# A layer of attention, state-space mixing and 32 routed experts: experts placed by token count, weights gathered by place

## The chip, the cores and the metric

The kernel runs on one core of a Trainium2 chip. The metric is device time in microseconds (us) of one execution; the time of a version is the median of its runs. Five engines work beside each other and meet at semaphores: TensorE (PE, matmuls, with its weight loads shown as PEld), VectorE (DVE), ScalarE (ACT), GpSimd (POOL) and SyncE (SP). Transfers (DMAs) are issued from the queues of SP, ACT and POOL and run on 16 shared DMA engines. Matmul results land in PSUM[...]; other tiles lie in SBUF, 128 partitions wide.

## The reference, cut to what matters

The layer adds three blocks to `x` (256 tokens x 512): attention over 4096 context tokens and itself, a state-space mixer, and a feed-forward block with a shared expert and 32 routed ones. The change lies in the routed part:

```python
scores = jax.nn.sigmoid(x @ gate_w)                      # 256 x 32
topk_w, topk_i = jax.lax.top_k(scores, 6)
topk_w = topk_w / (jnp.sum(topk_w, axis=-1, keepdims=True) + 1e-20)
combine = jnp.sum(jax.nn.one_hot(topk_i, 32) * topk_w[..., None], axis=1)
g = jnp.einsum('td,edf->tef', x, wg)                     # wg, wu: 32 x 512 x 192
u = jnp.einsum('td,edf->tef', x, wu)
act = jax.nn.silu(g) * u
routed = jnp.einsum('tef,efd,te->td', act, wd, combine)  # wd: 32 x 192 x 512
shared = jax.nn.silu(x @ sg) * (x @ su) @ sd
return routed + shared
```

A token uses 6 of the 32 experts, so 1536 rows of work are spread unevenly over them. All values are f32.

## The kernel before

**Places.** Every expert has a place of 128 rows in a scratch tensor `xg` in device memory, expert `e` at row `128 e`. Experts are worked on in 16 pairs, `n` = 0 to 15, pair `n` holding experts `2n` and `2n + 1`. If an expert has over 128 tokens, the flag `crowded` sends the kernel through a second pass over all places (the `Else` arm at its end).

**Routing.** For each token tile `t` of 128, `route` (L988) computes gate scores, the six chosen experts and the 0/1 matrix `mask`; `rows_of` (L1017) multiplies `mask` with a triangle of ones, which gives each token its rank within its expert, and from that the row it goes to. `scatter` (L1010) then sends the tile's normalised rows to `xg` with six indirect DMAs from POOL. Tile 0 goes through this while tile 1 is still in the mixer. `picks` (L1033) builds selection matrices for the first four experts (`HEAD`), whose rows are picked on PE by `ps_pick` (L1302) instead of going through `xg`. `shares` (L1039) computes the flag and the normalised weights. The shared expert (`shared_hidden`, `shared_down`) runs on PE between these steps.

**Weights.** A pair has three pieces of 128 x 1536 f32 (768 KiB): gate and up of the first expert, of the second, and both down weights. The host lays them out as one array `pairs`. Fifteen slots (five pairs, `NHELD`) hold them; they are SBUF tiles of earlier stages, filled as these come free. `load_piece(p)` (L1079) issues piece `p` from SP's queue into slot `p % 15`, as soon as PE has finished with the piece before.

**The loop over pairs** (L1337) issues, in step `n`: `gate_up(n)`, the loads of pair `n + 5`'s two gate pieces, `fetch(n + 2)` (two 128 x 512 row blocks from `xg`, on SP's queue), `turn(n + 1)` (eight 128 x 128 transposes and a copy), `down(n - 1)` with the store of its rows to `ye` from ACT's queue, the load of pair `n + 4`'s down piece, and `turn_hidden(n)`. In `gate_up`, each expert takes four f32 matmuls of 128 rows x 384 columns, then SiLU on ACT and two products on VectorE. An expert's hidden width is 192 = 128 + 64: the two 64-wide rests of a pair share one 128-wide transpose, and in `down` (L1288) they are multiplied as two matmuls of 64 partitions each.

**The end.** The last six experts (`TAIL`, pairs 13 to 15) don't go through `ye`. `weights_back` builds matrices `spread` that carry a token's weight for each place row, `spread_hidden` multiplies the hidden rows with them, and `down_into` sums the results in two PSUM banks, `total`. The results of the other experts come back by twelve indirect DMAs from POOL (`gather`, L1192) and are added on VectorE (`add`). Two last adds (L1378) and two stores end the kernel.

**What sets the order.** The program text gives an order, and a scheduler moves instructions within it as their operands become ready; each engine then runs its own stream in order. A wait therefore holds back all that is queued behind it on that engine. Clearing `xg`, `ye` and `ye2` (L515) is done during attention, in seven portions on SP's queue, with transfers pinned in program order.

Of the kernel before, what the change touches and what calls it, by code (L numbers as in the profile page):

```python
# [11 lines left out]
FP = mybir.dt.float32  # L12
# [42 lines left out]
NHELD = 5  # L55
HEAD = 4
TAIL = 6
ROUNDS = L // P
# [9 lines left out]
def perceiver_layer(ctx: ExitStack, tc: tile.TileContext, a: dict, out: bass.AP):  # L68
# [49 lines left out]

    xg = tc.dram_tile((ROUNDS * NE * P, DM), FP, name="xg")
    ye = tc.dram_tile(((NE + 1) * P, DM), FP, name="ye")  # L120
    ye2 = tc.dram_tile(((NE + 1) * P, DM), FP, name="ye2")
# [12 lines left out]
    def layer(ctx, bounded):  # L134
# [16 lines left out]
        most = keep.tile([1, 1], FP, name="most")  # L151
# [363 lines left out]
        def clear(n):  # L515

            per = -(-ROUNDS * NE // (NC - 1))
            e0, e1 = n * per, min((n + 1) * per, ROUNDS * NE)
            zeros(xg[e0 * P:e1 * P, :].rearrange("(e p) d -> p e d", p=P),
                  xn[:, 0:1, :].to_broadcast([P, e1 - e0, DM]))  # L520
            if n == 0:
                for y in (ye, ye2):
                    zeros(y[(NE - TAIL) * P:, :].rearrange("(e p) d -> p e d", p=P),
                          xn[:, 0:1, :].to_broadcast([P, TAIL + 1, DM]))
# [452 lines left out]
        def routing_memory():  # L977
            r = carve(lacc[:, 1], (P,), (P,), (NE,), (NT, NE), (NT, NE), (NT, NE), (NT, NE), (NT, NE), (NT, 8), (NT, 8),
                      (NT, TOPK), (NT, TOPK), (NT,), (NT * TOPK, NE), (FT, L))
            names = ("iota", "before", "first", "gate", "ev", "mask", "rank", "dst", "m8", "idx", "rowf", "w8", "den", "hot", "act")  # L980
# [3 lines left out]
            V.tensor_scalar(m["first"], m["iota"][:, 0:NE], float(P), None, ALU.mult)  # L984

# [31 lines left out]
        def rows_of(t):  # L1017

            mask, rank, dst, hot = m["mask"], m["rank"][:, t, :], m["dst"][:, t, :], m["hot"][:, t]
# [4 lines left out]
            V.tensor_copy(rank, pr)  # L1024

            V.tensor_scalar(dst, rank, float(P), float((NE - 1) * P), ALU.is_ge, ALU.mult)
            V.tensor_tensor(dst, dst, rank, ALU.add)
            V.tensor_tensor(dst, dst, m["first"], ALU.add)
            V.tensor_tensor(hot, hot, dst.unsqueeze(1).to_broadcast([P, TOPK, NE]), ALU.mult)
            V.tensor_reduce(m["rowf"][:, t, :], hot, AX.X, ALU.add)  # L1030
            V.tensor_copy(row[:, t, :], m["rowf"][:, t, :])
# [7 lines left out]
        def shares():  # L1039

            pr = bank("ps_most")[:, 0:NE]
            for t in range(NT):
                TE.matmul(pr, ones, m["mask"][:, t, :], start=(t == 0), stop=(t == NT - 1))
            V.tensor_reduce(most, pr[0:1, :], AX.X, ALU.max)
            V.tensor_scalar(crowded, most, float(P), None, ALU.is_gt)
# [32 lines left out]

        def load_piece(p):  # L1079
            if p < 3 * NP:  # L1080
                slots_of[p] = slots[p % (3 * NHELD)]
                nc.sync.dma_start(slots_of[p], a["pairs"][p // 3, p % 3])
# [80 lines left out]
        rows_of(0)  # L1163
# [3 lines left out]
        scatter(0)  # L1167
        load_into(wvc, wkc, ctx0)
        load_into(*w_out)
        pick, = carve(m["kv", 1], (NT * HEAD, P))  # L1170
        pick = pick.rearrange("p (t e) r -> p t e r", t=NT)
        picked, = carve(m["kv", 0], (KD, HEAD, P))
        turn()
        shared_down(0)
        route(1)
        product, turn = shared_hidden(1)
        product()
        rows_of(1)
        scatter(1)
        for t in range(NT):  # L1180
            picks(t)
        shares()
        turn()
        shared_down(1)
        actx.close()

# [21 lines left out]
        class Rounds:  # L1208


            def __init__(self, ctx, weights):
                pool = lambda name, bufs, **kw: ctx.enter_context(tc.tile_pool(name=name, bufs=bufs, **kw))
                self.r, self.weights = 0, weights
                self.e2, self.e4 = pool("e2", 2), pool("e4", 4)
                self.ps_x, self.ps_gu = pool("ps_x", 2, space=PSUM), pool("ps_gu", 2, space=PSUM)
                self.ps_t, self.ps_ye = pool("ps_t", 1, space=PSUM), pool("ps_ye", 3, space=PSUM)
                self.rows, self.xgT, self.hid, self.hidT, self.done = {}, {}, {}, {}, {}

            def fetch(self, n):
                for i in range(2):  # L1220
                    self.rows[n, i] = self.e4.tile([P, DM], FP, tag="xg", name="xg_sb")
                    r0 = (self.r * NE + 2 * n + i) * P
                    nc.sync.dma_start(self.rows[n, i], xg[r0:r0 + P, :])
# [245 lines left out]
```

## Time and profile before

| | value | how to read it |
|---|---|---|
| median of 3 runs | 1013.92 us | 1013.66 to 1014.13 |
| the profiled execution | 1013.77 us | its own device time |
| its span | 1012.0 us | first to last instruction, 9057 of them |
| PE busy | 992.4 us, 98% | matmuls overlap and their ends are modelled: busy is not peak |
| PE weight loads busy | 477.8 us, 47% | beside the matmuls |
| DVE, ACT, POOL busy | 498.6, 391.7, 152.6 us | 49%, 39%, 15% of the span |
| mean granted PE clock | 0.999 | 1 is full speed |
| DMA | 131.94 MB, mean 130 GB/s | in the expert stage, 860 to 940 us, 352 to 365 GB/s |

A line of the timeline or of the chain of waits gives the start in us from the span's start, the length in us, the engine, the line of the kernel, the operation, what it writes and reads, and how many instructions are merged in it; in brackets stands the idle time before it and who ended it. "SPq" and "ACTq" are DMA issues. The attention part fills the first 740 us, the mixer the time to about 820, routing and the shared expert the time to about 840, and the pairs of experts the rest.

### The profile page before, as it was taken

The numbers are of one execution on the slowest core, as the hardware profiler recorded it, in microseconds if no ns is written. First come the engines' busy times: TensorE is split into PE (matmuls) and PEld (weight loads), VectorE is DVE, ScalarE is ACT, GpSimd is POOL, SyncE is SP. The second block draws the span as 40 slices with busy tenths as digits, with TensorE's granted clock in tenths as the row PEclk, the third lists the DMA queues.
The fourth block names the chain that finished last, engine by engine and source line by source line (L and its number), as shares of the span: only waits on it lengthen the run. The fifth ranks groups of instructions, "written<-read, shape, count | busy, mean of one in ns | idle before, by whom it ended". The sixth has DMA issues, their size and how long they took to land.

```text
span 1012.0 us, 9057 instructions
## 1 busy us (share of the span) xinstructions
PE 992.4 (98%) x2786; PEld 477.8 (47%) x2786; DVE 498.6 (49%) x976; ACT 391.7 (39%) x862; POOL 152.6 (15%) x155
## 2 busy tenths in 40 slices
PE   7999999999999999999999999999999999999997
PEld 3444444444444444444444444444656554555554
DVE  4455555454454454454544544575886653322124
ACT  3645444343443443443443434432444431222210
POOL 4343002001101101100201200000132322000013
PEclk9999999999999999999999999999999999999999
DMA  9635045132222313303304203500254358999823
GB/s 335 214 64 169 0 146 197 32 97 80 52 47 99 83 32 114 84 17 129 83 8 138 64 0 84 156 11 0 94 189 155 114 208 321 350 358 367 310 98 116
DMA packets 136556, 131.94 MB, mean 130 GB/s; under 512 B 80401, under 2 KB 99762, under 8 KB 135346
## 3 DMA queue, kind: packets, MB, share of 16 engines
q1 hardware_dynamic: 129392, 115.71, 36.0%
q0 software_dynamic: 2208, 8.39, 2.3%
q10 hardware_dynamic: 4898, 7.16, 1.9%
q8 instruction: 24, 0.39, 0.1%
q14 instruction: 34, 0.28, 0.1%
HBM read 90.86 MB, written 40.39 MB: 130 GB/s over the span
## 4 chain that ended last, share of the span: by engine, by line
PE 95%; DVE 1%; ACT 1%; POOL 1%; DMA 1%; issue 0%; SPq 0%; ACTq 0%
PE oT L586 23%; PE scT L561 23%; PE ps_kv L358 17%; PE ps_egu L212 8%; PE ps_self L212 3%; PE ps_ye L1285 2%; PE ps_v L212 2%; PE ps_o L782 2%; PE total L1276 2%; PE ps_xbc L212 1%; PE ps_ye L1288 1%; PE ps_k L212 1%; PE xgTp L1230 1%; PE ps_out L972 1%; PE ps_yd L912 1%; DMA wkv<-in_wk_ctx_dram 1%
## 5 line engine op out<-in xcount | busy, mean ns | idle before, releaser
L577 DVE TENSOR_TENSOR lacc<-lacc,prT 128x512 f32<-128x512 f32 x256 | 182.7, 715 | 240.5 <-ACT prT L567 239.7
L567 ACT ACTIVATE prT<-scT,bq,rk 128x512 f32<-128x512 f32 x256 | 198.8, 777 | 254.7 <-PE scT L561 242.1
L561 PE MATMUL scT<-qT,kT 128*128 128x512 f32 x536 | 270.9, 592 | 0.0
L586 PE MATMUL oT<-prT,v 128*128 128x512 f32 x528 | 268.0, 592 | 0.9 <-ACT prT L567 0.9
L586 PEld LDWEIGHTS oT<-prT,v 128*128 128x128 f32 x528 | 100.1, 190 | 127.2 <-issue 115.0
L561 PEld LDWEIGHTS scT<-qT,kT 128*128 128x128 f32 x536 | 101.2, 190 | 124.6 <-issue 122.2
L190 POOL TENSOR_TENSOR rk<-pv,mhalf 128x4 f32<-128x4 f32 x32 | 32.3, 1010 | 371.1 <-DVE pv L189 371.1
L1245 DVE TENSOR_TENSOR hid<-si,ps_egu 128x128 f32<-128x128 f32 x32 | 9.2, 288 | 95.7 <-ACT si L1243 94.2
L358 PE MATMUL ps_kv<-wkv,fast 128*128 128x512 f32 x112 | 53.4, 592 | 0.0
L248 ACT ACTIVATE sq<-kraw 128x128 f32<-128x128 f32 x128 | 35.6, 278 | 45.2 <-DVE kraw L376 43.2
L358 PE MATMUL ps_kv<-wkv,ctx 128*128 128x512 f32 x112 | 52.8, 592 | 0.0
L358 PE MATMUL ps_kv<-fast,fast 128*128 128x512 f32 x112 | 52.6, 592 | 0.0
L592 DVE TENSOR_TENSOR oacc<-oT,oacc 128x512 f32<-128x512 f32 x64 | 43.7, 683 | 0.0
L1291 ACT COPY y_sb<-ps_ye 128x512 f32<-128x512 f32 x26 | 15.2, 585 | 48.8 <-PE ps_ye L1288 43.0
L358 PEld LDWEIGHTS ps_kv<-wkv,fast 128*128 128x128 f32 x112 | 21.3, 190 | 26.8 <-issue 26.8
L358 PEld LDWEIGHTS ps_kv<-fast,fast 128*128 128x128 f32 x112 | 21.3, 190 | 26.8 <-issue 21.8
L358 PEld LDWEIGHTS ps_kv<-wkv,ctx 128*128 128x128 f32 x112 | 21.3, 190 | 26.8 <-issue 23.7
L1198 POOL DMA_INDIRECT yk<-ye,row_y x12 | 12.8, 1064 | 139.0 <-DVE hid L1246 135.7
L1243 ACT ACTIVATE si<-ps_egu 128x192 f32<-128x192 f32 x32 | 10.6, 331 | 58.5 <-PE ps_egu L212 58.5
L376 DVE TENSOR_TENSOR kraw<-ps_kv,fast 128x256 f32<-128x256 f32 x42 | 17.9, 425 | 28.2 <-PE ps_kv L358 28.2
L782 PE MATMUL ps_o<-wo,qT 128*128 128x512 f32 x64 | 28.8, 592 | 0.0
L212 PE MATMUL ps_self<-wq,xT 128*128 128x512 f32 x64 | 28.1, 592 | 0.0
(298 smaller groups left out, 1120.9 us busy)
## 6 DMA issues: line engine op xcount, KB each, us to landing
xg<-xn SPq DMA_DIRECT2D x6, 2560.0 KB, 9.9
w_in<-in_pairs_dram SPq DMA_DIRECT2D x14, 768.0 KB, 6.6
ctx<-in_ctxT_dram SPq DMA_DIRECT2D x7, 1024.0 KB, 9.2
kd<-tr SPq DMA_DIRECT2D x112, 64.0 KB, 2.1
kT<-kd SPq DMA_DIRECT2D x28, 256.0 KB, 2.7
xg_sb<-xg SPq DMA_DIRECT2D x28, 256.0 KB, 6.0
ye<-y_sb ACTq DMA_DIRECT2D x26, 256.0 KB, 7.0
wkv<-in_pairs_dram SPq DMA_DIRECT2D x6, 768.0 KB, 6.5
```

What stands on the lines that cost most here:

```text
L190: return G.tensor_tensor(dst, v[:, :n], mhalf[:, :n], ALU.pow)
L212: TE.matmul(ps, lhs(k), rhs_of(k), start=(k == 0), stop=(k == KD - 1))
L248: S.activation(sq[:, h, :], raw[:, h, :], AF.Square, accum_out=ss[:, h:h + 1])
L358: TE.matmul(ps, lhs(k), rhs(k), start=(start and k == 0), stop=(k == 1), skip_group_check=True)
L561: TE.matmul(sc, kT[:, g, i * P:(i + 1) * P], qT[:, t, heads4(g), :].rearrange("p h q -> p (h q)"), start=True, stop=True)
L567: S.activation(pr, sc, AF.Exp, bias=shift, scale=SCALE if r is None else r[:, i, g:g + 1])
L577: V.tensor_tensor(la, la, pr, ALU.add)
L586: TE.matmul(outs[g, t], v[:, i, g * HD:(g + 1) * HD], pr, start=(n == 0), stop=last)
L592: V.tensor_tensor(ov, outs.pop((g, t)), ov, ALU.add)
L782: TE.matmul(m["ps_o", t], aT[:, t, h, :], wo[j][:, h % 4, :], start=(h == 0), stop=(h == NH - 1))
L1276: TE.matmul(total[t], h[:, j, t * P:(t + 1) * P], wd[:, j, :], start=(first and j == 0), stop=(last and j == 2))
L1285: TE.matmul(ps[i], h[:, i, :], wd[:, i, :], start=True, stop=False)
```

## The change

Ten experts (0 to 9, `FIXED`) keep their places, two pairs' worth of which are picked on PE as before. The other 22 are sorted by token count on the chip. The ten with most tokens take wide places of 128 rows (pairs 5 to 9), the other twelve narrow places of 64 rows (pairs 10 to 15), two of which share one block of 128 rows. Only now is it known which expert sits where, so the weights of pairs 5 to 15 are gathered by place with indirect DMAs from POOL, five per pair, and the host lays weights out by expert. A narrow pair is computed in halves of 64 stationary columns that write the lower and the upper half of one PSUM bank. A token beyond 64 in a narrow place, or 128 in another, raises `crowded`; the second pass's memory grows accordingly.

Both tiles' rows depend on the counts of all tokens, so all twelve scatters now follow `places` and `rows`, which come after the second tile's routing; `route(1)` is put ahead of `shared_down(0)`. Pair 2's `turn` is put behind `down(0)`. The constants, the sizes of `xg`, `ye` and `ye2`, and the clears follow the new places: thirteen blocks in a portion where it was ten, and a single block each for `ye` and `ye2` where it was seven.

```diff
+FIXED = 2 * NHELD
+WIDE = FIXED + 10
+HALFP = P // 2
-ROUNDS = L // P
+ZROW = WIDE * P + (NE - WIDE - TAIL) * HALFP
+MAIN = ZROW + TAIL * HALFP
...
+        def places():
+            mask, first, pos, key, keys, at, less, over = (m[n] for n in ("mask", "first", "pos", "key", "keys", "at", "less", "over"))
+            few, n, low = slice(0, NE), NE - FIXED, slice(FIXED, NE)
+            pc = bank("ps_count")
+            for t in range(NT):
+                TE.matmul(pc[:, 0:NE], ones, mask[:, t, :], start=(t == 0), stop=(t == NT - 1))
+            pp = bank("ps_count2")
+            for t in range(NT):
+                TE.matmul(pp[few, 0:16], mask[:, t, :], ones[:, 0:16], start=(t == 0), stop=(t == NT - 1))
+            V.scalar_tensor_tensor(keys, pc[:, 0:NE], float(NE), m["iota"][:, 0:NE], ALU.mult, ALU.subtract)
+            V.tensor_scalar(keys, keys, float(2 * NE), None, ALU.add)
+            V.scalar_tensor_tensor(key[few], pp[few, 0:1], float(NE), m["p"][few], ALU.mult, ALU.subtract)
+            V.scalar_tensor_tensor(key[few], key[few], float(2 * NE), m["free"][few], ALU.add, ALU.mult)
+            V.tensor_scalar(at[few, 0:n], keys[few, low], key[few], None, ALU.is_gt)
+            V.tensor_reduce(pos[few], at[few, 0:n], AX.X, ALU.add)
+            V.tensor_scalar(at[few], ident[few, few], pos[few], None, ALU.mult)
+            V.tensor_scalar(less[few, 0:n], m["iota"][few, 0:n], pos[few], None, ALU.is_equal)
+            ps = bank("ps_place")
+            TE.matmul(ps[:, 0:NE], ones[few], at[few], start=True, stop=True)
+            TE.matmul(ps[:, NE:NE + n], number[few], less[few, 0:n], start=True, stop=True)
+            V.tensor_copy(at, ps[:, 0:NE])
+            V.tensor_copy(expert, ps[:, NE:NE + n])
...
+        def rows():
+            rank, dst = m["rank"], m["dst"]
+            by_tile = lambda ap: ap.unsqueeze(1).to_broadcast([P, NT, NE])
+            V.tensor_tensor(dst, rank, by_tile(m["less"]), ALU.add)
+            V.tensor_scalar(dst, dst, float(P), None, ALU.is_ge)
+            V.tensor_tensor(dst, dst, by_tile(m["over"]), ALU.mult)
             V.tensor_tensor(dst, dst, rank, ALU.add)
+            V.tensor_tensor(dst, dst, by_tile(m["first"]), ALU.add)
+            for t in range(NT):
+                hot = m["hot"][:, t]
+                V.tensor_tensor(hot, hot, dst[:, t].unsqueeze(1).to_broadcast([P, TOPK, NE]), ALU.mult)
+                V.tensor_reduce(m["rowf"][:, t, :], hot, AX.X, ALU.add)
+                V.tensor_copy(row[:, t, :], m["rowf"][:, t, :])
...
+        def gather_weights(slot, n, j):
+            def rows(out, src, c):
+                G.indirect_dma_start(out=out, out_offset=None, in_=src.rearrange("e p n -> (e p) n"),
+                                     in_offset=bass.IndirectOffsetOnAxis(ap=place[:, c:c + 1], axis=0))
+            s = 2 * n - FIXED
+            if j < 2:
+                rows(slot, a["gu"], s + j)
+            else:
+                for i in range(2):
+                    rows(slot[:, i * DM:(i + 1) * DM], a["down"], s + i)
+                rows(slot[:, 2 * DM:], a["down_rest"], NE - FIXED + s // 2)
...
-                nc.sync.dma_start(slots_of[p], a["pairs"][p // 3, p % 3])
+                (load_weights if p < 3 * NHELD else gather_weights)(slots_of[p], p // 3, p % 3)
...
-        rows_of(0)
+        ranks(0)
         product, turn = shared_hidden(0)
         mamba_out(1)
         product()
-        scatter(0)
...
         turn()
+        route(1)
         shared_down(0)
-        route(1)
         product, turn = shared_hidden(1)
         product()
-        rows_of(1)
-        scatter(1)
+        ranks(1)
+        places()
+        rows()
+        for t in range(NT):
+            scatter(t)
         for t in range(NT):
             picks(t)
         shares()
+        weight_rows()
         turn()
         shared_down(1)
...
+            def gate_up_halves(self, n):
+                ps = self.ps_gu.tile([P, 2 * FE], FP, tag="gu", name="ps_egu")
+                xT = self.xgT.pop((n, 0))
+                w = [self.weights[3 * n + i].rearrange("p (k n) -> p k n", k=KD) for i in range(2)]
+                for k in range(KD):
+                    for i in range(2):
+                        TE.matmul(ps[self.half(i)], xT[:, k, self.half(i)], w[i][:, k, :], start=(k == 0), stop=(k == KD - 1))
+                si = self.e2.tile([P, FE], FP, tag="si", name="si")
+                S.activation(si, ps[:, 0:FE], AF.Silu)
+                hid = self.hid[n] = self.zeroed[n % 2]
+                V.tensor_tensor(hid[:, 0:P], si[:, 0:P], ps[:, FE:FE + P], ALU.mult)
+                for i in range(2):
+                    h = self.half(i)
+                    self.done[n] = V.tensor_tensor(hid[h, P + i * REST:P + (i + 1) * REST], si[h, P:FE], ps[h, FE + P:], ALU.mult).ins
...
+            def down_halves(self, n, to):
+                wd = self.weights[3 * n + 2].rearrange("p (j n) -> p j n", j=3)
+                h = self.hidT.pop(n)
+                ps = self.ps_ye.tile([P, DM], FP, tag="ye", name="ps_ye")
+                for i in range(2):
+                    TE.matmul(ps[self.half(i)], h[:, 0, self.half(i)], wd[:, i, :], start=True, stop=False)
+                TE.matmul(ps, h[:, 1, :], wd[:, 2, :], start=False, stop=True)
...
+            def spread_halves(self, n, by):
...
+                for i in range(2):
+                    TE.matmul(whole[i][:, 0, :], h[self.half(i), 0:P], by[self.half(i)], start=True, stop=True)
+                TE.matmul(whole[1][:, 1, :], h[:, P:2 * P], by, start=True, stop=True)
...
-                main.gate_up(n)
+                wide = 2 * n < WIDE
+                (main.gate_up if wide else main.gate_up_halves)(n)
...
-                if FIRST <= n + 1 < NP:
+                if FIRST <= n + 1 < NP and n + 1 > FIRST:
                     main.turn(n + 1)
                 if 0 < n <= LAST:
-                    main.down(n - 1, ye)
+                    (main.down if 2 * (n - 1) < WIDE else main.down_halves)(n - 1, ye)
+                    if n + 1 == FIRST:
+                        main.turn(n + 1)
```

Three more functions are used above. `ranks` is the first half of the old `rows_of`. `weight_rows` turns the sorted experts into row numbers for the gathers, in five steps on VectorE. `turn_hidden_halves` transposes two 128-wide blocks instead of three; the hidden tiles of narrow pairs are two zeroed tiles whose unused corners stay zero. In `weights_back` the matrices are built for two narrow places together: six transposes where there were twelve, after a selection of ranks and weights by place on VectorE.

## The prediction

> **What bounds the kernel now.** I began with the busy table and the 40 slices: TensorE (PE) is busy 98% of the span at a granted clock of 0.999, but the DMA row also stands at 8 and 9 in slices 33 to 37, so an average can't say which of the two sets the pace of the expert stage. The windows by stage settle it. The columns of the next line are the stretch, its length, busy time of PE, weight loads, VectorE (DVE), ScalarE (ACT) and GpSimd (POOL), then clock, DMA share and GB/s.
>
> ```profile
> 880.00:900.00 20.00, 20.00 (x83) 11.43 (x83) 7.61 (x22) 4.38 (x11) 0.00 (x0) 1.00 0.97 352
> ```
>
> PE has no hole, the DMA engines hardly one, POOL does nothing. The chain that ended last, followed in order of time, gives one pair of experts:
>
> ```profile
> 861.77 5.16 PE ps_egu L212 x16
> 866.93 0.87 PE xgTp L1230 x8
> 867.81 1.72 PE ps_ye L1285 x4
> 869.53 1.06 PE ps_ye L1288 x4
> 870.59 0.48 PE hidTp L1252 x3
> ```
>
> The chain never leaves PE: 9.29 us a pair (861.77 to 871.06), and the same lines return up to pair 12. Each f32 matmul is two records, so 5.16 us is 16 of 0.322 us. In the same 9.29 us the queues move 3 weight pieces of 768 KiB, two row blocks in and two out of 256 KiB, 3.41 MB: 367 GB/s, what the DMA engines give at a share near 1. Yet PE waits for none of it, because weights come five pairs ahead: pair 15's gate pieces are issued at 940 and 943, and its gate-up starts at 989, a lead of over 40 us.
>
> The third view is the timeline around the routing, where the path leaves PE:
>
> ```profile
> 821.45 0.96 POOL L1013 DMA_INDIRECT xg<-xn,row  x1 [0.30 <-issue]
> 822.44 0.58 POOL L190 TENSOR_TENSOR rs<-pv,mhalf 128x1 f32<-128x1 f32 x1
> ...
> 843.86 0.96 POOL L1013 DMA_INDIRECT xg<-xn,row  x1 [0.30 <-issue]
> 848.96 1.75 SPq L1223 DMA_DIRECT2D xg_sb<-xg  x4
> ```
>
> The layernorm's factor stands behind a scatter of the first token tile; the last scatter ends at 844.82 and rows may be fetched 4.1 us later. PE first needs them at 857.48, so there is cover.
>
> **Does the routing fit the places?** Routing the reference's own inputs gives counts that sum to 1536. Of the 22 sorted experts the tenth largest has 63 rows, so the largest narrow one has 43; no fixed or wide one has over 103. Nothing overflows 64 or 128, and the second pass isn't taken.
>
> **The six narrow pairs (10 to 15), PE alone.** The halves of gate-up have half the stationary columns each and write different halves of one bank. No row of the trace splits the array by columns; the nearest splits it by rows, L1288: 4 records of 512 columns in 1.06 us, where L1285 takes 1.72 for four whole ones. Two perfect lanes would take 0.86, so a change of tiling costs 0.20.
> - Gate-up: 5.16 becomes 2.58 + 0.20, and some 0.07 for the lanes' offset: 2.85. Saved 2.31 x 6 = 13.9.
> - Row transposes (one block, not two): 0.87 to 0.435, x 6: 2.6.
> - Down, pairs 10 to 12: 1.72 + 1.06 = 2.78 becomes 1.06 for the halves and 0.86 for the shared rest: 1.92. x 3: 2.6.
> - Hidden transposes: two for three, 0.16 x 3: 0.5.
> - Spreading, pairs 13 to 15: 1.06 + 0.86 = 1.92 becomes 0.43 + 0.20 + 0.43 = 1.06. x 3: 2.6.
> - Spread transposes: six for twelve of 1.6 us: 0.8.
> Sum: **23.0 us**.
>
> [...] both column halves use all rows. The trace's row: whole loads of 190 ns ("PEld LDWEIGHTS" of L212) use all rows too, and their matmuls still follow each other every 0.322 us. [...] With no concurrency at all it is 5.16 + 0.20. I take the row. Below 2.58 two lanes can't go.
>
> Other engines keep up: in a narrow step of some 5.5 us ACT has 0.33 + 0.58 and under 0.48 for the hidden copy, DVE about 1.4 (0.68 + 0.29 + two of 0.21). The next pair's transposed rows have the down product and the hidden transposes, 2.2 us, to be copied in 0.68.
>
> **Routing.** `places` adds two counts and a placement on PE in place of `ps_most` (4 records, 0.45 us): 12 records for 4, +0.9. Its vector work, all after the second tile's mask, is some 18 dependent steps at 0.18 to 0.22 on 32 columns before `rows`, which has five steps on 64 columns and two times 0.85 (L1029 to L1031). I make it 6.1 us and 1.5 of PE round trip: 7.6 from mask to last row, where it was 832.36 to 837.27, 4.9. Against that, route(1) now goes ahead of shared_down(0) (2.84), and no scatter stands before the layernorm factor on POOL: VectorE hands it over at 821.07 and POOL starts at 822.44, so 1.3 us go and PE's wait at L1064 (0.9) with it, -1. So rows are ready at 837 to 840, I say 838.5.
>
> Then **all twelve scatters** stand in one run: 12 x 1.26 = 15.2 us, ending 853.7 instead of 844.8. Plus 4.1 the fetch is at 857.8, plus 2.6 to 3.5 landing (2.6 is the fastest fetch of the trace) the rows are there at about 861. Besides, VectorE between 828 and 838 must do some 11 us in 10, with the picks that `ps_pick` waits for: +1 (0 to 3). The change moves pair 2's transposes behind down(0). Gate-up(0), at 846.62 before, comes at 846.62 + 0.9 - 1 + 1 = 847.5, and 5.16 + 5.64 + 2.78 later, at 861.1, the transposes are due: level with the rows. Where two chains meet, either can be late: **stall 1 us**, between 0 and 5 (rows ready at 842.5, nothing gained by the reordering).
>
> **Weights move from SP's to POOL's queue.** Per pair five gathers, each blocking on its slot; behind a blocked one stand only further weight gathers, since the y gathers come after the last of them. SP keeps the row fetches, no longer behind 768 KiB loads (median landing 6.0). The first gathers wait for the scatters, 853.7 instead of 850.8: inside the lead. The near row is the y gather:
>
> ```profile
> 980.48 0.99 POOL L1198 DMA_INDIRECT yk<-ye,row_y  x1 [135.66 <-DVE hid L1246]
> 981.78 0.96 POOL L1198 DMA_INDIRECT yk<-ye,row_y  x1 [0.30 <-ACT si L1243]
> 983.05 0.95 POOL L1198 DMA_INDIRECT yk<-ye,row_y  x1 [0.31 <-issue]
> ```
>
> They start every 1.3 us without waiting for each other's landing: 5 x 1.27 = 6.3 us a pair, under 9.29. Were POOL's time to grow with the bytes (6 KB rows against 2 KB), it is 2 x 3.2 + 3 x 1.27 = 10.2 a pair, 112 us for eleven, done at 967. Pair 10 starts at 937.57 + 0.9 - 1 + 1 + 1 = 939.5, and the steps after it take 6.4, 5.5, 5.5, 6.3 and 9.5 by the numbers above: pair 15 needs its weights at 973. [...] The row shows the starts overlapping, so I count nothing.
>
> The clears grow from ten blocks to thirteen (3.4 MB), the first shrinks from 6.2 to 3.9; attention, which shows no wait for 6.2, hides them. POOL's two memsets of hidden tiles (nearest row: its 128x512 add, 1.27 us), `weight_rows` and the four extra steps of `shares` come after the scatters' rows and ahead of the first gather only, in its lead.
>
> **The end.** After down(12) at 974.26, PE has 32.06 us left. Of these go 2 x 2.31 (pairs 14, 15), 0.43 and three spreads of 0.86: 24.4 left. The y gathers hang on the same point: copy and store 5.3 (one block's copy fewer than 6.2), 16.1 of issue, 2 to land, 0.9 to add: 24.3. They were 6.5 us early; now they are level with PE, +0.7 (0 to 2).
>
> **Sum.** -23.0 + 0.9 - 1 + 1 + 1 + 0.7 = -20.4: span 991.6. Around the profiled span lie 1.77 us (1013.77 against 1012.0), and that execution stands 0.15 below the median of 1013.92. Forecast **993.5 us**.
>
> **Rivals.**
> - *The halves overlap, but badly, or the stall is long* ([...] rows at 842.5 or later, +4 and more: 998 to 1004). For: no row with column halves; DVE is full around 830. Against: the row-split row. 20%.
> - *No concurrency by columns*: gate-up 5.36, down 2.78, a spread 1.49. Left are 2.6 + 0.5 + 1.3 + 0.8 - 1.2 = 4.0 against 2.6 of the other terms: 1012.5, about nothing. Against it is again L1288, which does run two at once. 4%.
> - *Gathered weights bind: slower.* Place: POOL's queue from 853.7 on. Eleven pairs, 25.95 MB, must be in by pair 15's gate-up; before, that stood at 989. It gets slower than before when the gathers bring under 192 GB/s (25.95 MB in 135 us), 12.3 us a pair. [...] For it: these gathers are not in the trace, 55 of them are new. Against: the overlapping starts; q0 moved 8.39 MB in 2.3% of the span, at full rate. 8%.
> - *It doesn't do what it says*, the overflow pass running after all: the counts exclude it. 1%.
> The forecast itself, 987.5 to 998, has 67%.
>
> Bounds for the range: perfect lanes (-23.0, -1.6 in the gate-ups, -1.2 in down and spread), no stall, no VectorE delay, no late end, and the full 1.3 at the layernorm give -26.2: 987.5. The second case reaches 1004, and outside lie about 15%. Faster 0.87, same 0.03, slower 0.10; a difference under 0.2% (2 us) can't be told from none here.
>
> **What would show it.** Right: L212's gate-up records of pairs 10 to 15 fill about 2.9 us instead of 5.16; a narrow step of 5.4 to 5.6; a PE wait of 0 to 2 us before pair 2's L1230 whose releaser is the fetch of `xg`; pairs 3 to 9 still at 9.29; POOL starts 1.3 us apart. Wrong: gate-up near 4 or 5; PE waiting on a DMA into a weight slot from pair 5 on; a wait of 5 us or more before pair 2; a last `x_sb` add that waits for `yk` by more than 2 us.

## The result, and the profile after

| | before | after |
|---|---|---|
| median | 1013.92 us (1013.66 to 1014.13) | 1008.28 us (1007.29 to 1008.99) |
| ratio, 95% interval | | 0.9943, 0.9929 to 0.9958 |
| profiled execution, its span | 1013.77, 1012.0 us | 1007.29, 1005.6 us |
| mean granted PE clock | 0.999 | 0.993 |

The change gains 5.6 us, where 20.4 were forecast. By the two profiled spans the sum reads: up to the start of pair 3's gate-up +12.1 us (871.06 became 883.17), from there to the end of the last `total` -20.8 (135.24 became 114.44), and from the last add to the end +2.3 (5.68 became 7.96). Forecast were +1.9, -23.0 and +0.7.

The wide pairs are as they were, and the narrow ones did shrink. The chain that ended last, in order of time, start and length first: a wide pair, then a narrow one.

```profile
893.12 5.16 PE ps_egu L216 x16
898.28 0.87 PE xgTp L1338 x8
899.16 1.72 PE ps_ye L1430 x4
900.88 1.06 PE ps_ye L1433 x4
901.94 0.48 PE hidTp L1412 x3
...
954.90 2.73 PE ps_egu L1353 x16
957.63 0.59 PE xgTp L1338 x4
958.22 1.01 PE ps_ye L1375 x4
959.22 1.06 PE ps_ye L1376 x2
960.28 0.22 PE hidTp L1366 x2
```

A wide pair takes 9.29 us as before, a narrow one 5.60, and both stay on PE: no gathered weight is waited for. The window by stage of the wide pairs agrees; POOL, idle there before, is now busy for half the time, and DMA still stands at 0.97.

```profile
880.00:900.00 20.00, 20.00 (x79) 11.26 (x78) 5.86 (x16) 4.43 (x10) 9.71 (x11) 1.00 0.97 345
```

What went wrong lies ahead of pair 3. The timeline of POOL around the routing, last scatters and first weight gathers:

```profile
843.83 1.10 POOL L1020 DMA_INDIRECT xg<-xn,row  x1 [7.38 <-DVE xc L1473]
...
857.88 0.96 POOL L1020 DMA_INDIRECT xg<-xn,row  x1 [0.30 <-issue]
859.15 0.99 POOL L1158 DMA_INDIRECT v<-in_gu_dram,place  x1 [0.30 <-issue]
860.44 0.96 POOL L1158 DMA_INDIRECT w_in<-in_gu_dram,place  x1 [0.30 <-issue]
```

The first scatter starts at 843.83, not 838.5, and 0.3 us behind the twelfth stands the first weight gather, ahead of the fetch of pair 2's rows, which goes out at 860.87. PE's timeline shows what that does:

```profile
867.78 1.09 PE L1338 MATMUL xgTp<-ident,xg_sb 128*128 128x128 f32 x4 [5.36 <-DMA xg_sb<-xg]
870.91 1.12 PE L1338 MATMUL xgTp<-ident,xg_sb 128*128 128x128 f32 x4 [2.04 <-DMA xg_sb<-xg]
```

Each block's transposes wait for the block's fetch, 7.4 us together. The two fetches landed 6.9 and 10 us after the first of them was issued, at 860.87. The windows over that stretch (busy time of PE, weight loads, VectorE, ScalarE, POOL, then clock, DMA share, GB/s) add a second price:

```profile
865.00:868.00 3.00, 0.21 (x1) 0.25 (x2) 0.00 (x0) 0.00 (x0) 2.04 (x3) 0.50 1.02 348
...
871.00:874.00 3.00, 3.00 (x10) 2.39 (x11) 0.69 (x1) 0.48 (x1) 0.00 (x0) 0.50 1.03 415
874.00:877.00 3.00, 3.00 (x9) 1.62 (x9) 0.14 (x1) 0.33 (x1) 0.26 (x1) 0.84 1.04 409
```

The clock falls to half while PE waits and stays there until 875, some 4 us after PE has taken up work again, so pair 2's gate-up takes 6.37 us instead of 5.16. The DMA share stands at 1.02 to 1.04 in these lines: the fetch is not idle, it shares.

The end has its own surprise. The last instruction groups belong to the program's end; name, count, then shortest, median and longest duration in ns. Before, then after:

```profile
L1465 POOLq DRAIN  x3: 40/107/2280, 1002.8 to 1011.7; - x3
```

```profile
L1619 POOLq DRAIN  x3: 45/107/6757, 997.9 to 1005.3; - x3
```

POOL's longest drain grew from 2280 to 6757 ns. Before, it began at 1002.8 and had ended 1.2 us ahead of the last add (1006.32). Now it begins at 997.9, 0.3 us behind the start of the last add, and the program ends 0.9 us behind its end. The y gathers, which the forecast set level with PE, were early: they ran 975.03 to 991.03 and the last of them was added by 994.4, ahead of the last totals. They touched PE once: `hidS` stood on VectorE behind an add that waited for its gather, and PE waited 0.4 us for it:

```profile
986.63 1.98 PE L1421 MATMUL total<-kT,hidS 128*128 128x512 f32 x4 [0.37 <-DVE hidS L1392]
```

### The profile page after: what moved, and what is told of

It is laid out like the page before. It is cut to its first block, busy times and chain, and to the rows that moved or that the text cites. A ratio compares the mean times of both kernels' runs of the same rounds, so it can differ in the third digit from the quotient of the medians.

```text
span 1005.6 us, 8991 instructions
## 1 busy us (share of the span) xinstructions
PE 975.4 (97%) x2749; PEld 461.7 (46%) x2749; DVE 498.0 (50%) x992; ACT 387.3 (39%) x853; POOL 206.8 (21%) x214
## 4 chain that ended last, share of the span: by engine, by line
PE 91%; DMA 3%; DVE 2%; POOL 1%; ACT 1%; issue 1%; SPq 0%; POOLq 0%; DVEq 0%; ACTq 0%
PE oT L590 23%; PE scT L565 23%; PE ps_kv L362 17%; PE ps_egu L216 4%; PE ps_self L216 3%; PE ps_v L216 2%; PE ps_o L786 2%; PE ps_ye L1430 2%; PE ps_k L216 1%; PE ps_xbc L216 1%; PE ps_out L976 1%; PE ps_egu L1353 1%; PE ps_sgu L216 1%; PE xgTp L1338 1%; PE total L1421 1%; DMA xg_sb<-xg 1%
## 5 line engine op out<-in xcount | busy, mean ns | idle before, releaser
L1405 DVE TENSOR_TENSOR hid<-si,ps_egu 128x128 f32<-128x128 f32 x20 | 5.8, 288 | 62.6 <-ACT si L1403 62.6
L356 POOL TENSOR_TENSOR fast<-ctx 128x512 f32<-128x512 f32 x7 | 9.5, 1363 | 113.1 <-PE ps_kv L362 94.2
L601 DVE RECIPROCAL lacc<-ps_l 128x512 f32<-128x512 f32 x8 | 26.8, 3348 | 0.1
L362 PE MATMUL ps_kv<-fast,ctx 128*128 128x512 f32 x56 | 26.3, 593 | 0.0
## 6 DMA issues: line engine op xcount, KB each, us to landing
xg<-xn SPq DMA_DIRECT2D x6, 3328.0 KB, 11.6
```

Of the source, the lines that this page charges most:

```text
L362: TE.matmul(ps, lhs(k), rhs(k), start=(start and k == 0), stop=(k == 1), skip_group_check=True)
L601: V.reciprocal(rl, ps)
```

## The experiments

Two theories at the start. **A**: the weights' gathers, which start ahead of pair 2's fetch, take its share of the DMA engines. **B**: the rows are simply too late, by the routing's own length. Each expectation below was written before its run and names its own two theories, A and B. The edits are against the changed kernel unless said otherwise. Between profiled executions the start of the routing shifts: PE takes up the shared expert's first product (`ps_sgu`) between 818.2 and 820.7 us, so lengths are compared below and not times of day; for the routing they count from the second tile's top-8, the choice of its six experts. "Before" was run beside each group: 1014.17 us (e1 to e4), 1013.98 (e5 to e8), 1013.87 (e9, e10), 1013.74 (e11, e12).

### e1: the gathers held until the rows are there

```diff
-                for j in range(2):
-                    load_piece(3 * (n + NHELD) + j)
+                if n == 0:
+                    main.fetch(2)
+                    for i in range(2):
+                        held = G.tensor_copy(landed[:, i:i + 1], main.rows[2, i][:, 0:1]).ins
+                with tc.issue_after(held):
+                    for j in range(2):
+                        load_piece(3 * (n + NHELD) + j)
```

> The changed kernel, with the weight gathers of steps 0 and 1 held on POOL until pair 2's rows have landed (two one-column reads of them on POOL stand ahead of the gathers). Theory A, the gathers started 1.7 us before the row fetch and took its bandwidth: the fetch, issued at about 861, lands in 3 to 4 us instead of 6.9 and 10, PE's wait falls from 7.4 to some 2 us, its clock stays at 1, and the time is about 1000.5. Theory B, the late scatters alone made the wait: fetch landing and time as in the changed kernel, 1008.

Measured: 1002.04 us (1000.77 to 1004.32), ratio 0.9884 (0.9865 to 0.9902). POOL's timeline; the fetches were issued from 862.61 on:

```profile
865.37 0.18 POOL L1497 COPY landed<-xg_sb 128x1 f32<-128x1 f32 x1 [4.78 <-DMA xg_sb<-xg]
866.00 0.18 POOL L1497 COPY landed<-xg_sb 128x1 f32<-128x1 f32 x1 [0.44 <-DMA xg_sb<-xg]
866.84 1.00 POOL L1158 DMA_INDIRECT v<-in_gu_dram,place  x1 [0.66 <-PE ps_ye L1430]
```

Both blocks were there in 2.8 to 3.4 us, with twelve scatters just ahead and no gather beside them. So the forecast's landing time was right for a fetch without gathers, and the gathers took the rest. PE's wait for rows is gone as well, but in part by luck: in this execution PE came to pair 2's transposes late itself.

```profile
867.43 1.09 PE L1338 MATMUL xgTp<-ident,xg_sb 128*128 128x128 f32 x8
```

In the changed kernel they were due at 862.42. Here the routing started 1.7 us later, `ps_pick` took 8.83 us instead of 7.13, at a clock of 0.87 and 0.79 between 840 and 850 (more on that at the end), and a hole of 1.67 us stood in pair 1's gate-up. With the late start alone PE would have been there at 864.1 and the rows at 865.4 and 866.0; e6 shows what is left of the wait in an execution without these delays.

### e2: pair 2's rows picked on PE

Selection matrices as for the first four experts serve pair 2 as well, so that nobody waits for `xg` until pair 3.

```diff
+                    for k in range(KD):
+                        for t in range(NT):
+                            TE.matmul(ps[:, k, :], xn[:, t, k * P:(k + 1) * P], pick[:, t, i, :],
+                                      start=(t == 0), stop=(t == NT - 1))
```

> The changed kernel, with pair 2's rows picked on PE by selection matrices (16 more f32 matmuls of 128 columns, about 3.5 us for 0.9 of transposes) instead of being fetched, so that the first fetched rows are needed 9 to 10 us later. If the wait for pair 2's rows and the clock behind it are what ate the gain (7.4 us of wait, some 2.5 of clock), the time falls by 7 to 8, to about 1000.5, gathers and scatters being as late as before. If something else holds pair 2 or 3 (weights, another engine), the wait moves to pair 3 and the time stays above 1005.

Measured: 1004.39 us (1003.73 to 1005.11), ratio 0.9909 (0.9893 to 0.9926). Between the two: no wait for rows, but the picks cost 4.1 us of PE, and the two halves of pair 2's gate-up began with holes of 1.20 and 1.27 us, while the copies of the picked rows stood in VectorE's queue behind the spread matrices. Buying the wait off with PE time is dear: of the 9.5 us of wait and slow clock, 3.9 are left as gain.

### e3: vector work that the rows don't need behind them

```diff
-        shares()
-        weight_rows()
+        with tc.issue_after(rows_done):
+            shares()
+            weight_rows()
```

> The changed kernel, with the vector work that nobody waits for (shares, weight_rows, the matrices of weights_back) held behind the last step of rows. If that filler put between the steps of the chain made the rows late, they are ready at about 841.5 instead of 843.8, the scatters and the fetch move with them, and the time falls by 2 to 3, to 1005.5. If the chain's own latency set it, the time stays within 0.5 of 1008.

Measured: 1007.11 us (1005.03 to 1011.0), ratio 0.9938 (0.9921 to 0.9956). The first scatter started 15.0 us after the second tile's top-8, against 15.8 in the changed kernel. The fillers made the rows late by 0.8 us of the 5.3, no more.

### e4: the gathered weights loaded from SyncE

The weights of pairs 5 to 15 come in expert-number order from SP's queue; 26 software DMAs are left, as in the kernel before: those of POOL's queue, twelve scatters, twelve y gathers and two loads of `lm`. The changed kernel has 55 more, the weights' gathers.

```diff
-                (load_weights if p < 3 * NHELD else gather_weights)(slots_of[p], p // 3, p % 3)
+                load_weights(slots_of[p], p // 3, p % 3)
```

> The changed kernel, with the weights of pairs 5 to 15 loaded from SP's queue in the order of the experts' numbers; left out is that they follow the sorted places. Theory A: SP runs its queue in order, the loads stand behind or beside the blocked row fetch, the fetch has the DMA engines nearly alone, and the time is about 1001. Theory B: as the changed kernel, 1008. Also the stretch from the last vector add to the end of the span (8.0 us, 5.7 before the change): if the gathers on POOL lengthened it, it is 5.7 here.

Measured: 1004.54 us (1002.35 to 1005.43), ratio 0.9901 (0.9885 to 0.9918). PE's wait did not go, it halved and moved: 1.3 us at pair 2 and 2.6 at pair 3, whose fetch stood behind two 768 KiB loads on SP's queue. PE was late in this execution as it was in e1 (`ps_pick` 8.83 us, a hole of 1.69), which hides some of the wait at pair 2. From last add to end it took 5.62 us, as before the change.

### e5: the kernel before with late scatters, first try

```diff
-        scatter(0)
...
         rows_of(1)
-        scatter(1)
+        for t in range(NT):
+            scatter(t)
```

> The kernel before with tile 0's six scatters moved behind tile 1's row numbers, so that all twelve run in one piece (from about 837.5 us, 15 us long, as in the changed kernel), with no gathered weights beside or behind them. Theory A (late scatters alone cost little; it is the weights' gathers that delay the fetch): the fetch of pair 2's rows is issued about 2 us after the last scatter's end at 852.5 and lands in about 3 us, at 857.5 to 858, against a first row transpose due at 857.6: a wait of 0 to 1 us, 1014 to 1015 us. Theory B (a fetch right behind twelve scatters lands in 7 to 10 us whatever runs beside it): TensorE waits 4 us or more, about 1018 us or more.

Measured: 1013.71 us (1013.22 to 1014.11), ratio 0.9997 (0.9989 to 1.0006). That looks like theory A, but POOL's timeline shows no test of it:

```profile
825.72 0.96 POOL L1013 DMA_INDIRECT xg<-xn,row  x1 [0.31 <-issue]
837.45 0.96 POOL L1013 DMA_INDIRECT xg<-xn,row  x1 [10.77 <-DVE lacc L1311]
```

Six scatters still ended at 826.7: the scheduler starts them when their rows are known, wherever the call stands. e11 repeats it with a dependence that can't be moved.

### e6: held gathers, rows first, and the first shared add behind the mask

e1 and e3 together, and:

```diff
-        shared_down(0)
+        with tc.issue_after(mask_done):
+            shared_down(0)
```

> The changed kernel with three edits together: the gathers of steps 0 and 1 held behind pair 2's landed rows (as in e1), the vector work that the rows don't need held behind the rows (as in e3), and the first shared-expert add held behind tile 1's mask. Theory A (rows were also late because other vector work stood in their way, some 0.65 us of it measured in e3 and about 1.8 us by the add in the middle of the gates): the rows and the picks are ready about 2 us earlier than in e1 and TensorE's wait before the picks goes: about 1000 us. Theory B (the routing's own chain of dependent steps sets it, and the add's place is indifferent): 1002, as e1.

Measured: 1000.06 us (999.14 to 1004.38), ratio 0.9872 (0.9854 to 0.9890). `ps_pick` waits 0.8 us instead of 2.1, the clock stays at 1.00 from 836 to 880, and PE still waits 1.8 us for pair 2's rows:

```profile
863.72 1.22 PE L1341 MATMUL xgTp<-ident,xg_sb 128*128 128x128 f32 x8 [1.84 <-DMA xg_sb<-xg]
```

This is the price of late rows with the gathers held: 1.8 us where the changed kernel has 7.4. The first scatter came 15.0 us after the top-8, as in e3, so holding the add did nothing for the rows.

### e7: down weights from SyncE, 48 software DMAs

```diff
-                (load_weights if p < 3 * NHELD else gather_weights)(slots_of[p], p // 3, p % 3)
+                (load_weights if p < 3 * NHELD or p % 3 == 2 else gather_weights)(slots_of[p], p // 3, p % 3)
```

> The changed kernel, where only the gate-up weights are gathered by place and the down weights of pairs 5 to 15 are loaded from SyncE in expert-number order (so it leaves out sorting the down weights): 48 software DMAs instead of 81. Theory A (GpSimd's drain at the end grows with the number of software DMAs that the program issued, 82 ns each: 2.28 us at 26, 6.76 us at 81): the drain is 2.28 + 22 x 0.082 = 4.1 us and the span past the last add is about 2 us shorter than in the changed kernel. Theory B (the drain hangs on something else, such as the gathers of weights being there at all): it stays near 6.8 or falls to 2.3 us.

Measured: 1004.94 us (1001.79 to 1005.86), ratio 0.9904 (0.9888 to 0.9920). The group at the program's end:

```profile
L1619 POOLq DRAIN  x3: 45/107/4077, 997.6 to 1003.1; - x3
```

4.08 us, where 4.1 was expected from the count alone, and 5.69 us from last add to end instead of 7.96. PE's wait for rows stayed at 7.5 us. In these four programs the drain goes by the count of software DMAs: 2280, 4077 and 6757 ns at 26 (e4 and the kernel before), 48 and 81 (the changed kernel), which is 81 to 82 ns for each one more. It doesn't go by bytes: the 22 gate-up gathers of e7 carry two thirds of the weights and make up 40% of the growth.

### e8: the first shared add alone behind the mask

The same edit as in e6, alone.

> The changed kernel with one edit: the first shared-expert add is held behind tile 1's expert mask on VectorE, so it no longer stands between the top-8 and the match of the gates. Theory A (its wait for TensorE held the mask, and through it the rows and the picks, by up to 1.8 us): the first scatter starts 1 to 2 us earlier (842 instead of 843.8), TensorE's wait before the picks shrinks by as much: about 1006.5 us. Theory B (the mask's consumers are late for other reasons, such as TensorE reaching the ranks only behind the shared product): the first scatter moves by under 0.5 us, 1008 us as before the edit.

Measured: 1006.23 us (1001.91 to 1008.29), ratio 0.9917 (0.9893 to 0.9941). VectorE reached the mask's last step 1.1 us after the top-8 instead of 2.9, yet PE took up the ranks at the same distance:

```profile
827.54 0.20 DVE L1010 MAX8 lacc<-lacc 128x8 f32<-128x32 f32 x1
...
828.67 0.49 DVE L1015 TENSOR_REDUCE lacc<-lacc 128x32 f32<-128x192 f32 x1
...
834.02 0.18 DVE L1031 COPY lacc<-ps_rank 128x32 f32<-128x32 f32 x1
```

The copy of the ranks comes 6.5 us after the top-8, as in the changed kernel (827.99 and 834.48), and the first scatter 15.8, as there. So the mechanism is theory B's, and the 2 us that the median moved can't be put down to the add: the intervals of both kernels overlap.

### e9: ranks and places ahead of the shared product

On top of e6:

```diff
-        product, turn = shared_hidden(1)
-        product()
         ranks(1)
         places()
+        product, turn = shared_hidden(1)
+        product()
```

> The kernel of e6 with TensorE's ranks, counts and places of tile 1 written ahead of the shared expert's product instead of behind it. In e6 the mask was ready at 830.4 us, but TensorE reached the ranks only at 834.5, behind 4.7 us of that product, and the first scatter started 15.0 us after the second tile's top-8. Theory A (TensorE's order, not the vector steps, made the rows late): the first scatter starts about 11 us after the top-8, the fetch lands before TensorE asks for it and its wait of 1.8 us goes; against it stands a new hole of 0 to 2 us before the picks, since the shared expert's steps lose the cover of the ranks: 998 to 1000 us. Theory B (the dependent vector steps themselves set it): the first scatter stays 14 us or more behind the top-8 and the time stays at 1000 us or rises.

Measured: 999.62 us (998.05 to 1001.72), ratio 0.9863 (0.9846 to 0.9879). The first scatter starts 11.6 us after the top-8 (829.20 to 840.76), and no wait for rows is left. What made the rows late in the changed kernel and its variants up to e8 was PE's order: the ranks stood behind 4.7 us of shared product. The hole came too: `ps_pick` starts 14.8 us after the top-8 instead of 12.4 in e6, so the time hardly moved.

### e10: the same with the gathers not held

The order of e9 and the add of e8, without e1 and e3.

> The changed kernel with the add of e8 and the order of e9, but with the weights' gathers not held: they start right behind the last scatter and run beside the fetch of pair 2's rows. Theory A (the gathers delay the fetch by 4 to 7 us wherever it stands, and an earlier row chain only moves both): scatters and fetch come some 4 us earlier, the fetch still takes 6 us or more to land, and TensorE's wait falls from 7.4 to about 3.5 us: 1003 to 1005 us. Theory B (earlier rows are enough): the fetch lands in 3 us and the wait is gone: about 1000 us.

Measured: 1002.49 us (1000.69 to 1004.71), ratio 0.9897 (0.9878 to 0.9915). The gathers begin at 855.29 and the fetches at 857.01; the fetches of that stretch took 6.9 us at the median again, which is theory A. But PE did not wait at all, because it came later itself: `ps_shared` ran at a lowered clock (4.54 us instead of 2.84; 0.64 in the window 840 to 844), and pair 2's transposes were due only at 864.96. So an early fetch can be slow without cost where PE isn't there yet; whether it would cost with PE on time, as theory A has it, this profile can't show. It is of the shortest of the four executions; two others took 1004.09 and 1004.71 us, which is theory A's range, and have no profile.

### e11: the kernel before with late rows

The kernel before; the cast of tile 0's rows is held behind tile 1's, so all scatters run in one piece.

```diff
-        scatter(0)
...
-        rows_of(1)
-        scatter(1)
+        rows_done = rows_of(1)
+        with tc.issue_after(rows_done):
+            V.tensor_copy(row[:, 0, :], m["rowf"][:, 0, :])
+        scatter(0)
+        scatter(1)
```

> The kernel before again with all twelve scatters in one piece, which moving the calls alone did not bring about (in e5 the first tile's scatters stayed where they were): now the last cast of tile 0's row numbers is held behind tile 1's, so no scatter can start before about 837.5 us. No weight comes through GpSimd's queue here. Theory A (late scatters alone cost little): the last scatter ends near 852.7, the fetch goes out 2 us later and lands in 2.7 to 5 us, at 857.4 to 859.7, against a first row transpose due at 857.5: a wait of 0 to 2.2 us, 1013 to 1016 us. Theory B (a fetch right behind twelve scatters takes 7 to 10 us whoever shares the engines): TensorE waits 4 us or more, 1018 us or more.

Measured: 1019.63 us (1019.15 to 1020.66), ratio 1.0060 (1.0043 to 1.0076): slower by 6 us, on the side of theory B, but not for its reason. The issues on SP's queue, then PE's timeline:

```profile
854.11 0.33 SPq L1225 DMA_DIRECT2D xg_sb<-xg  x1
854.54 0.38 SPq L1082 DMA_DIRECT2D v<-in_pairs_dram  x1
855.02 0.37 SPq L1082 DMA_DIRECT2D w_in<-in_pairs_dram  x1
855.44 0.42 SPq L1225 DMA_DIRECT2D xg_sb<-xg  x1
```

```profile
856.94 0.63 PE L1232 MATMUL xgTp<-ident,xg_sb 128*128 128x128 f32 x4
861.55 1.11 PE L1232 MATMUL xgTp<-ident,xg_sb 128*128 128x128 f32 x4 [3.98 <-DMA xg_sb<-xg]
862.46 3.62 PE L1287 MATMUL ps_ye<-w_in,hidT 128*128 128x512 f32 x4
```

Two equal fetches, 1.3 us apart. The first has no weights ahead of it and is there in time, within 2.8 us. The second follows two 768 KiB loads and takes 6.1 us. The queue stood 14.0 us waiting for the scatters, and what had piled up behind left all at once. The 4.0 us of waiting then cost 2.6 more in a slow clock (on the chain 1.11 us for the four transposes instead of 0.44, 3.41 for `ps_ye` L1287 instead of 1.72, 1.32 for L1290 instead of 1.06); the clock stood at 0.50 in the window 860 to 864 and at 0.68 in 864 to 868, which puts its return at about 866.5. The time rose by 6 and not by 6.6 us, because this execution had reached the picks 0.6 us earlier than the kernel before. So the theory A of the start holds in a wider form: weights that move ahead of the fetch or beside it slow it, POOL's gathers or SP's own loads; and "late scatters cost little" was wrong where weights wait at the same gate.

### e12: counts ahead of the product, placement behind it

On top of e6, `places` is cut in two.

```diff
+        ranks(1)
+        places()
         product, turn = shared_hidden(1)
         product()
-        ranks(1)
-        places()
+        placed()
```

> The kernel of e6 with ranks and counts ahead of the shared expert's product on TensorE, but the placement matmuls behind it (in e9 they stood in the middle of it, and TensorE stood 2.3 us more before the picks than in e6, for 1.8 us won at pair 2). Theory A (what e9 lost was the cover of the shared expert's steps): most of that hole closes, the first scatter starts 12 to 13 us after the top-8, the fetch lands before it is due: 998 to 999 us. Theory B (the hole comes from VectorE's queue, which is as full in either order): 999.6 to 1000 us, as e9 and e6.

Measured: 999.92 us (998.89 to 1001.46), ratio 0.9860 (0.9844 to 0.9877). The first scatter came 11.8 us after the top-8 and the rows in time, but PE's waits have a new first line:

```profile
PE ps_pick L1456 <- DVE crowded L1118: 2.3, 1, 2.3
```

Theory B: VectorE's queue is full, and what is taken from one wait shows up in the next. The profile is of the longest of the four executions, in which `ps_pick` also took 8.68 us, where e6 and e9 have 7.13. e6, e9 and e12 stand within 0.5 us of each other and can't be told apart; each beats both kernels, by about 8 us against the change and 14 against the kernel before.

## Why the prediction was wrong

The forecast was 993.5 us in a range to 1004; the median is 1008.28. Its likeliest branch fell, and of the rivals "the stall is long" named the late rows, but not what slowed their fetch, and was priced at +4 and more, up to 1004. Term by term, in us of span:

| term of the sum | forecast | measured |
|---|---|---|
| narrow pairs | -23.0 | -20.8 |
| routing records, layernorm factor, VectorE's delay: start of `ps_pick` | +0.9 | +2.0 |
| stall before pair 2 | +1 | +7.4 |
| slow clock after it | not in the sum | +2.7 |
| the end | +0.7 | +2.3 |
| sum | -20.4 | -6.4 |

**Narrow pairs: right in kind.** Gate-up came at 2.73 us against 2.85. I took the row of the trace, in which loads over all rows don't hold up the matmuls, and it holds for half-width loads too. The two halves' loads start together, both over all rows:

```profile
955.20 0.14 PEld L1353 LDWEIGHTS ps_egu<-lacc,xgT 128*64 128x64 f32 x1 [0.18 <-issue]
955.21 0.14 PEld L1353 LDWEIGHTS ps_egu<-w_in,xgT 128*64 128x64 f32 x1
```

0.14 us each, and sixteen records fill 2.73 us without a gap, each pair of loads beside the matmuls of the pair before: gate-up saved 14.6 us where 13.9 were forecast. The 2.2 us that are missing are mis-sized smaller terms. The spreads saved 1.6 and not 2.6: I took 1.92 us for each of the three before, but only the first one, behind the row-split L1288, takes that; the other two take 1.72. And a spread takes 1.2 to 1.3 now, where I had 1.06.

```profile
987.37 0.86 PE hid_sp L1262 x4
988.23 0.86 PE rest_sp L1266 x4
```

The row transposes take 0.59 beside half-width matmuls, where I halved 0.87 to 0.435 (0.7 us in all), the shared rest of `down` (L1376) takes 1.06, where I had 0.86 (0.5 in all), and the wait for `hidS` adds 0.4. Against gate-up's extra 0.7 these make about 1.9; the other 0.3 is not placed.

**"Rows ready at 838.5": the first term that failed.** I priced mask to last row at 7.6 us, "some 18 dependent steps" and "1.5 of PE round trip". The first scatter started 12.4 us after the mask, at 843.83, later than the worst case that I had given (842.5). The round trip was most of the error: PE reached the ranks 2.3 us after the mask was there and the placement 1.1 us after its inputs, both times behind shared-expert matmuls. e8 shows that an earlier mask changes nothing, e3 that fillers cost 0.8, and e9 and e12 that another order on PE gives back 3.3 us (15.0 after the top-8 in e6, 11.6 and 11.8 there). A wrong term went the other way: I carried over 4.1 us from the last scatter to the fetch, and it was 2.0 (858.84 to 860.87).

**"Lands in 2.6 to 3.5", and "I count nothing" for the gathers: the second, and the larger.** I asked whether gathers keep up with PE (they do, 9.29 a pair stayed) and whether they start within their lead (they do), but not whom they meet when they start. The moved issues passed the fetch: twelve scatters hold both POOL and the fetch, and at the same moment 768 KiB pieces and two 256 KiB blocks are let go. Without gathers these blocks are there in 2.8 and 3.4 us (e1), and in 2.7 and 3.4 (e9: issued from 858.04, read by POOL at 860.73 and 861.40); beside gathers in 6.9 and 10, and in e10, which has e9's order but doesn't hold them, the fetches took 6.9 at the median; behind SP's loads one took 6.1 (e11). So weights beside it or ahead of it cost a fetch a factor of 2 to 3 in these runs; how the DMA engines share themselves out among the queues was not shown. Late rows alone cost 1.8 us (e6, near the forecast's 1); late rows together with weights let go beside them cost 7.4, and 4.0 in e11. The third case, early rows and gathers beside the fetch, is e10: no wait, but with a PE that was itself some 3 us later, so it is not shown what they would cost with PE on time.

**The slow clock: not in the sum.** A stall was counted at its own length. After 7.4 us of waiting, matmuls, transposes and gate-up cost another 2.7 us (0.6 of them in the first block's transposes, where PE would otherwise have waited; 2.1 behind the last wait); after 4.0 us in e11, 2.6. In the changed kernel the clock was 0.50 from 865 to 874, 0.84 to 877, 1.00 after. From the means of the windows (0.97 over 856 to 860 in e11 and over 860 to 865 in the changed kernel, 0.50 in the next) I estimate that the clock fell at 859.7 and 864.7, 2.2 and 2.3 us after PE had stopped (857.57 and 862.42). After the last wait it took 5.0 and 4.1 us of work to come back, by the same estimate.

**The end.** Of my 0.7 for the y gathers 0.4 came, by way of `hidS`, and the table has it in the narrow pairs: the copy and store ahead of the first gather took 3.6 us, where I had 5.3. What came in their place is POOL's drain, 2.3 us on the path. e4 and e7 take all of it away (5.62 and 5.69 us from last add to end): with 26 and with 48 software DMAs the drain is over before the end.

**What is left open.** e9's 999.62 is 6 us over the forecast. Narrow pairs (2.2) and the end (1.6) make up 3.8 of it. The rest lies before pair 3, in holes of PE that each order of the routing moved and none removed: 0.8 us before the picks and 1.8 at pair 2 in e6, 3.0 in four holes between the product and the picks in e9, 2.3 before the picks in e12. Up to 1.7 us of it is no hole of the routing at all: e9's execution had started the routing that much later than the kernel before (820.23 against 818.56), and why these starts differ is open. Whether an order without holes exists was not settled.

## What to carry to other kernels

When work is moved behind a late gate, list everything that the same gate lets go, in every queue, and look for the one small transfer among them that PE waits for: hold the large ones for the time it needs (2.8 to 3.4 us in e1). A chain of small steps through PE is priced by what PE has queued ahead of each of its steps, 4.7 us of shared product here, not by the steps. And a stall can cost more than its own length: waits of 4.0 and 7.4 us here cost 2.1 to 2.7 us of slow clock on top, and in some executions a wait of 2.07 or 2.08 cost 1.7.

## What the runs showed of the hardware

- **POOL's drain grew with the software DMAs of the program**: 2280 ns at 26, 4077 at 48, 6757 at 81, the same 6757 in e6 that issues as many. It is on the path where POOL comes to it late: in the changed kernel it begins 0.3 us behind the last add's start. 33 DMAs fewer (e7) took 2.3 us off the path.
- **Short holes can cut the clock as well.** A wait of 2.07 or 2.08 us before `ps_pick` left the clock at 1.00 in the changed kernel, in e2 and in e7 (7.13 us each), but in e1, e4 and e8 the sixteen records took 8.83 us after the same wait, and 8.68 in e12 after 2.35; in e1 the clock stood at 0.87 and 0.79. In e10 `ps_shared` took 4.54 us instead of 2.84 behind holes of 1.13 and 0.57. All of these are shorter than the wait of 4.0 us in e11 and the first one of 5.4 in the changed kernel. There is one profile of each run, so how often is open; the kernels with such holes also scatter more (1001.91 to 1008.29 in e8, against 1013.66 to 1014.13 before).
- **Matmuls next to half-width ones took a little longer**: four row transposes take 0.44 us between whole matmuls (pair 10's) and 0.59 behind a half-width gate-up; two records of 512 columns take 1.06 behind the halves of `down` (L1376), where two of four whole ones take 0.86. That the change of tiling is what costs was not tested apart.
